# Rotation sublayer of a two-layer decoder: from two batches of sixteen sequences to three batches, and later rotations

## The chip, the core and the metric

The kernel runs on one core of a Trainium2 chip. The core has a matrix engine (TensorE, "PE" in the profile, with its weight loads as "PEld"), a vector engine (VectorE, "DVE"), an activation engine (ScalarE, "ACT"), a general engine (GpSimd, "POOL") and SyncE ("SP"), which here does nothing but issue DMAs; ACT and POOL issue some DMAs as well. Every engine works through its own list of instructions in order, and waits where an instruction needs what another engine or a DMA has not yet delivered. The metric is the device time of one execution in microseconds (us), lower is better.

## What is computed

The input is 32 sequences of 128 tokens with 256 features, in f32, and every matrix product is done in f32. Two decoder layers follow each other. Layer 0 is an attention, a retention with a context, and a routed feed-forward with 8 experts. Layer 1 is the rotation sublayer that is changed here, then an attention with 16 heads, then a second routed feed-forward. The rotation sublayer, per sequence:

```python
h   = layernorm(x)                               # 128 x 256, per token
m   = h.mean(over the 128 tokens)                # one row of 256
om  = skew(m @ omega_proj_w.T + omega_proj_b)    # 64 x 64, antisymmetric
G   = I + om + om^2/2 + om^3/6                   # a rotation, by its series
vi  = m @ vq_in.T + b                            # 64; nearest of 64 codes by cosine
vq  = code[argmax] @ vq_out.T + b
y   = h + omega_mix * ((h[:, :64] @ G) @ omega_out_w.T + b) + vq_mix * vq
x   = x + rmsnorm(y) * norm_w
```

The attention after it needs, for each sequence, queries from `layernorm(x)` with the x that the rotation left; its keys and values come from the context and are ready long before.

## The kernel before

The 32 sequences lie in eight groups of four (`NG`, `GB`); group g is one tile x[g] of 128 tokens x 4 x 256. The stages follow each other: A and B (layer 0's attention and retention), C (layer 0's experts), then D and E together (rotation and attention), and F (layer 1's experts).

**Stage D** (`stage_d`, L1374) begins when stage C's last rows are out. It fetches what the experts made (1 MB for each group, L471, on SP) and the weights of omega in two halves of 2 MB (L1156, on SP). For each group `Dispatch.add` (L488, L489, DVE) sums them into x, and `Lie.measure` takes the layernorm statistics (L173 to L175 on DVE, the root on POOL at L146, a shift at L183). `Lie.means` (L1185) then takes the mean over tokens on PE: for each sequence and each half of the features one product with the 128 x 128 block of x as the weights and one column moving (L1194), and a product with ones for the shift (L1199). All this is done for half of the groups (16 sequences), and `Lie.omegas` (L1201) follows for that half: omega is 64 x 64 numbers a sequence, made in eight parts of 512 columns (L1220, weights 128 x 16), each copied out of PSUM by ACT (L1225) and written to a table in DRAM by SP (L1226); between the parts stand the steps that choose the code and add its row to the output weights `wob` (L1231 to L1273). The second half's means and parts are handed out one piece a step by a generator, `rest()`.

**Turned** (L1279) is the rotation of one group, and its parts are called in different steps: the constructor fetches omega from the table with the sequence index moved inward (L1286, SP), `norm` (ACT, L190), `head` (transposes on PE, L1336) and `square` (DVE L1308, L1309, then PE L1300), `cube`, `spin` (L1345), and `add`, which multiplies with `wob` (L1358), adds and normalises on DVE, ACT and POOL (L1360 to L1367) and adds the result to x (L1371).

**Group** (L1436) makes the queries of one group: its statistics, `norm` (ACT, into one of the two buffers with the tag "h"), `turn` (eight transposes, L239, and two copies), and `queries(h)` for each half h of the features: two products of 512 columns (L1456), an ACT copy (L1461), and eight DMAs on SP (L1464) that place 16 rows each in the tile qT. **Seq** is the attention of one sequence: `largest` (L1478, 16 products on qT, and DVE's maxima, L1485), `less` (L1491, L1493), `scores` (L1501, exponentials on ACT, L1502), `values` (L1509) and `back` (L1519, L1524, L1526).

**The order** around the change is PE's, written out by hand in `step(b)` (L1541), called for b = -13 to 32. Step b does `largest` of sequence b+1, then what is due of queries, turns, rotations and `rest`, then `values` of sequence b-1, `scores` of sequence b, `back` of b-1 and `less` of b+1. A part with the lag n is due for group G in step 4G+n. The other engines' lists come from the scheduler, which follows PE's order; SP's list too. The buffers with tag "h" are shared by the groups' norm, omega's copied parts, and others; there are two. Routing for stage F (`RouteF`: DVE's `rank` with L336 and L338, and `place` on PE with L354 and L355) joins from step 5 on. The lags before:

```python
for n in (-4, -3): ... q.queries(n + 4)          # one half h in each step
if q := due(groups, -5): q.turn()
for n, what in ((-9, "add"), (-10, "spin"), (-11, "cube"), (-12, "head"), (-12, "square")):
```

Of the kernel before, what the change touches and what calls it, by code (L numbers as in the profile page):

```python
# [28 lines left out]
P = 128  # L29
# [242 lines left out]
class Dispatch:  # L272
# [211 lines left out]
    def add(self, g, yg, behind=None):  # L484

        for i in range(0, GB, 2):
            x, y = self.k.x[g][:, i : i + 2, :], yg[:, i : i + 2]
            self.k.order(self.nc.vector.tensor_add(y[:, :, 0, :], y[:, :, 0, :], y[:, :, 1, :]).ins, behind)  # L488
            self.nc.vector.tensor_add(x, x, y[:, :, 0, :])  # L489
# [626 lines left out]

class Lie:
# [3 lines left out]
    def __init__(self, k, p1):  # L1121
        nc = k.nc
        self.k, self.nc, self.p1 = k, nc, p1
        self.w, self.line, self.stats, self.sums = {}, {}, {}, []

    def load(self):
# [5 lines left out]
        for name, shape in shapes.items():  # L1132
            self.w[name] = self.tile(shape, name)
            nc.scalar.dma_start(out=self.w[name], in_=k.ins[name])

# [33 lines left out]
    def length(self, v, n, name):  # L1169

        nc = self.nc
        sq = self.tile([n, OM], f"sq{name}")
        ss = self.tile([n, 1], f"ss{name}")
# [6 lines left out]
    def measure(self, g):  # L1180
        k = self.k
        st = k.stats(g, pool=self.p1, name=f"d_{g}")
        self.stats[g] = st + (k.shift(st, self.p1, f"d_{g}"),)

    def means(self, g):  # L1185

        k, nc = self.k, self.nc
        if g % (NG // 2) == 0:
            self.sums.append(k.bank([P, NC + 1, B // 2]))
        sums, st = self.sums[-1], self.stats[g]  # L1190
        for i in range(GB):
            b = g % (NG // 2) * GB + i
            for c in range(NC):
                nc.tensor.matmul(  # L1194
                    sums[:, c, b : b + 1], lhsT=k.x[g][:, i, c * P : (c + 1) * P], rhs=st[1][:, i : i + 1],
                    start=True, stop=True,
                )
        b -= GB - 1
        nc.tensor.matmul(sums[:, NC, b : b + GB], lhsT=k.deal.ones, rhs=st[2], start=True, stop=True)  # L1199

    def omegas(self, half, pd):  # L1201


        k, nc, w = self.k, self.nc, self.w
        N, HB = 8, B // 2
        tile = lambda shape, name: self.tile(shape, f"{name}{half}")
        mu = tile([P, HB], "mu")
        sums = self.sums[half]
        nc.scalar.activation(mu, sums[:, NC], AF.Copy, scale=1.0 / P)
        hm = tile([P, NC, HB], "hm")  # L1210
        nc.vector.scalar_tensor_tensor(
            hm, sums[:, 0:NC], 1.0 / P, mu.unsqueeze(1).to_broadcast([P, NC, HB]), ALU.mult, ALU.add
        )
        line = self.line[half] = pd.tile([HB, OM, OM], F32, name=f"d_line{half}")

        def part(n):
            po = k.bank([HB, N, OM], "s")
            i = n * N % (OM // 2)
            for c in range(NC):
                nc.tensor.matmul(  # L1220
                    po, lhsT=hm[:, c, :], rhs=self.wu[:, 2 * n * N // OM, c, i : i + N, :],
                    start=c == 0, stop=c == NC - 1,
                )
            rows = k.lnp.tile([HB, N, OM], F32, name="d_rows", tag="h")
            self.copied = nc.scalar.copy(rows, po).ins  # L1225
            nc.sync.dma_start(out=line[:, n * N : (n + 1) * N], in_=rows)  # L1226

        yield part(0)
        pT = k.bank([OM, HB])
        for c in range(NC):  # L1230
            nc.tensor.matmul(pT, lhsT=w["vin"][:, c, :], rhs=hm[:, c, :], start=c == 0, stop=c == NC - 1)  # L1231
        viT = tile([OM, HB], "viT")
        nc.vector.tensor_scalar_add(viT, pT, w["vibc"])
        pvi = k.bank([HB, OM])
        for c in range(NC):
            nc.tensor.matmul(pvi, lhsT=hm[:, c, :], rhs=w["vin"][:, c, :], start=c == 0, stop=False)
        k.bias_mm(pvi, "D_vib", HB)
        vi = tile([HB, OM], "vi")
        nc.vector.tensor_copy(vi, pvi)
        rn = self.length(vi, HB, f"v{half}")  # L1240
        if half == 0:
            self.codes()
        yield part(1)
        psc = k.bank([HB, OM])
        nc.tensor.matmul(psc, lhsT=viT, rhs=self.cbT, start=True, stop=True)
        sc = tile([HB, OM], "sc")
        nc.vector.tensor_scalar_mul(sc, psc, rn)
        best = tile([HB, 1], "best")
        nc.vector.tensor_reduce(best, sc, AX.X, ALU.max)
        nc.vector.tensor_scalar(sc, sc, best, -float(OM), ALU.is_equal, ALU.mult)  # L1250
        nc.vector.tensor_add(sc, sc, w["iota"])
        nc.vector.tensor_reduce(best, sc, AX.X, ALU.min)
        nc.vector.tensor_scalar(sc, sc, best, None, ALU.is_equal)
        yield part(2)
        yield part(3)
        yield part(4)
        ph = k.bank([OM, HB])
        nc.tensor.transpose(ph, sc, k.ident[0:HB, 0:HB])
        hot = tile([OM, HB], "hot")
        nc.vector.tensor_copy(hot, ph)  # L1260
        yield part(5)
        pcode = k.bank([OM, HB])
        nc.tensor.matmul(pcode, lhsT=w["code"], rhs=hot, start=True, stop=True)
        vo = tile([OM, 2 * HB], "vo")
        nc.gpsimd.memset(vo, 0.0)
        nc.vector.tensor_sub(vo[:, 0:HB], pcode, viT)
        nc.vector.tensor_add(vo[:, 0:HB], viT, vo[:, 0:HB])
        yield part(6)
        pvc = k.bank([P, D])
        own = slice(OM + 2 * half * HB, OM + 2 * (half + 1) * HB)  # L1270
        nc.tensor.matmul(pvc[own], lhsT=vo, rhs=w["vout"], start=True, stop=False)
        k.bias_mm(pvc[own], "D_vob", 2 * HB)
        self.known = nc.vector.scalar_tensor_tensor(  # L1273
            w["wob"][own], pvc[own], w["mix"][own, 1:2], w["wob"][own], ALU.mult, ALU.add
        ).ins
        yield part(7)


class Turned:  # L1279


    def __init__(self, lie, g, pool):
        self.lie, self.k, self.nc, self.g, self.pool = lie, lie.k, lie.nc, g, pool
        self.om = self.full("om")
        half, first = divmod(g * GB, B // 2)
        self.fetched = self.nc.sync.dma_start(  # L1286
            out=self.om[0:OM], in_=lie.line[half][first : first + GB].rearrange("b i j -> i b j")
# [17 lines left out]
    def square(self):  # L1305
# [3 lines left out]
        nc.vector.tensor_mul(om, om, over(w["sign"]))  # L1309
# [64 lines left out]
def stage_d(k, lie, pool, pd, room):  # L1374


    half = NG // 2
    weights = lie.weights(pool)
    ygs, last = {}, None

    def fetch(g):
# [601 lines left out]
```

## Time and profile before

| | us |
|---|---|
| median of 17 runs (lowest, highest) | 1670.62 (1667.23, 1677.04) |
| the profiled execution, by its own time | 1672.54 |
| its span, first to last instruction | 1670.80 |
| stage C's last product ends | 1013.1 |
| `largest` of sequence 0 begins (step -1) | 1133.3 |
| `largest` of sequence 7 begins (step 6) | 1200.85 |
| PE busy, whole span | 1441.9 (86%) |
| PE busy from 1013 to 1133 | 89.3 of 120.0 |
| PE busy from 1133 to 1200.85 | 52.4 of 67.85 |
| the four steps 10 to 13, and 14 to 17 | 40.61 and 40.24 |

The page's views name a line of the kernel, an engine, and "out<-in" by the program's tile names. In a timeline the columns are the start in us, the duration in us, the engine and line, the operation, and how many instructions were merged; what stands in brackets is how long the engine had been idle before, and which line of which engine ended that. "PEclk" is the TensorE clock granted, as a share of full speed.

### The profile page before, as it was taken

What the parts mean: (1) busy time and instruction counts of PE and PEld (TensorE: products, weight loads), DVE (VectorE), ACT (ScalarE), POOL (GpSimd) and SP (SyncE); (2) the same over time, 40 slices, a digit from 0 to 9 for tenths busy, and PEclk for the clock granted to TensorE, in tenths of its full rate; (3) what the DMA queues carried; (4) which work ended last, traced back from release to release, by engine and by line L of the source; (5) the groups of instructions that cost most, each with busy time, mean ns of one, the idle gap of its engine ahead of it and who ended that gap; (6) DMA issues with size and microseconds to landing.
All of it is one profiled execution on the core that took longest, in us unless ns stands there. A gap on an engine that the chain in (4) does not pass through costs nothing.

```text
span 1670.8 us, 27093 instructions
## 1 busy us (share of the span) xinstructions
PE 1441.9 (86%) x9161; PEld 958.5 (57%) x9161; DVE 930.6 (56%) x3005; ACT 593.7 (36%) x1524; POOL 603.6 (36%) x621
## 2 busy tenths in 40 slices
PE   6999799999998479999999995796998887878873
PEld 4555577776677446666666664453555544456762
DVE  6666446777778533333333324544767776554566
ACT  2544333334434022222222221143675543433431
POOL 2111126667768721111111114121223543375553
PEclk8999999999999689999999996777999977789997
DMA  9991099911000921111111106300000121043486
GB/s 335 335 335 38 22 309 303 297 43 40 27 20 32 384 67 46 47 48 45 45 45 45 48 29 266 118 9 23 23 14 26 40 96 38 20 136 112 142 264 233
DMA packets 139947, 189.90 MB, mean 114 GB/s; under 512 B 14394, under 2 KB 118148, under 8 KB 137764
## 3 DMA queue, kind: packets, MB, share of 16 engines
q1 hardware_dynamic: 123188, 148.32, 29.3%
q0 software_dynamic: 13296, 36.52, 6.0%
q10 hardware_dynamic: 3328, 3.33, 0.6%
q8 instruction: 76, 1.25, 0.3%
q14 instruction: 59, 0.48, 0.1%
HBM read 69.54 MB, written 112.30 MB: 109 GB/s over the span
## 4 chain that ended last, share of the span: by engine, by line
PE 65%; DVE 14%; issue 6%; ACT 5%; POOL 5%; DMA 3%; SPq 1%; another core or an unknown queue 1%; POOLq 0%; DVEq 0%; ACTq 0%
PE ps L1068 13%; PE ps L1088 7%; PE ps L156 6%; PE ps L664 3%; PE ps L1501 2%; PE ps L1694 2%; PE ps L1710 2%; PE ps L881 2%; PE ps L897 2%; PE ps L239 2%; PE ps L1081 2%; PE ps L151 2%; DVE ln_st L173 2%; PE ps L840 1%; DVE b_sim L887 1%
## 5 line engine op out<-in xcount | busy, mean ns | idle before, releaser
L1068 PE MATMUL ps<-c_up,c_xT 128*128 x568 | 268.1, 595 | 0.0
L342 POOL DMA_INDIRECT r_ys<-c_yb,r_toi x71 | 67.8, 955 | 353.5 <-DVE r_w L460 313.2
L1068 PEld LDWEIGHTS ps<-c_up,c_xT 128*128 128x128 f32 x568 | 102.9, 191 | 73.6 <-issue 69.1
L1088 PE MATMUL ps<-c_down,c_hid 128*128 x568 | 134.8, 380 | 0.9 <-DVE c_hid L1083 0.9
L1088 PEld LDWEIGHTS ps<-c_down,c_hid 128*128 128x128 f32 x568 | 107.4, 190 | 47.2 <-issue 17.7
L887 DVE TENSOR_TENSOR b_sim<-ps,b_decay 128x512 f32<-128x512 f32 x128 | 79.8, 684 | 80.0 <-PE ps L881 48.5
L146 POOL TENSOR_TENSOR b_rs<-b_var,mhalf 128x16 f32<-128x16 f32 x32 | 93.5, 2922 | 82.9 <-DVE b_var L915 79.8
L1093 ACT ACTIVATE c_yb<-ps,r_w 128x256 f32<-128x256 f32 x71 | 33.7, 474 | 219.0 <-PE ps L1088 219.0
L1083 DVE COPY c_hid<-ps 128x512 f32<-128x512 f32 x71 | 49.1, 691 | 101.4 <-PE ps L1081 101.4
L342 POOL DMA_INDIRECT g_ys<-f_yb,g_toi x78 | 76.1, 975 | 63.0 <-DVE g_to L447 46.6
L146 POOL TENSOR_TENSOR ln_rs<-ln_ve,mhalf 128x4 f32<-128x4 f32 x40 | 40.7, 1020 | 133.3 <-DVE ln_ve L175 133.3
L1485 DVE TENSOR_REDUCE e_pad<-ps 128x4 f32<-128x512 f32 x128 | 82.4, 682 | 11.2 <-PE ps L1478 5.4
L1502 ACT ACTIVATE e_e<-ps 128x512 f32<-128x512 f32 x128 | 66.9, 603 | 46.2 <-PE ps L1501 46.1
L173 DVE BATCH_NORM_STATS2 ln_st<-x 128x6 f32<-128x256 f32 x192 | 74.9, 407 | 10.3 <-DMA x<-in_x_dram 5.5
L1076 DVE TENSOR_TENSOR c_su<-ps,c_su 128x512 f32<-128x512 f32 x71 | 49.1, 692 | 55.3 <-PE ps L1068 55.3
L1531 POOL TENSOR_TENSOR x<-x,e_t 128x256 f32<-128x256 f32 x32 | 23.2, 726 | 142.7 <-DVE e_t L1526 142.6
L1074 ACT ACTIVATE c_su<-ps 128x512 f32<-128x512 f32 x71 | 42.4, 598 | 86.8 <-PE ps L1068 86.8
L342 POOL DMA_INDIRECT r_xs<-c_h,r_rowi x64 | 63.9, 998 | 21.9 <-issue 15.2
L342 POOL DMA_INDIRECT g_xs<-f_h,g_rowi x64 | 62.8, 981 | 21.3 <-issue 16.0
L1694 PE MATMUL ps<-f_rw,f_xT 128*128 x312 | 52.5, 294 | 12.5 <-issue 11.2
L1710 PE MATMUL ps<-f_rw,f_hb 128*128 x156 | 51.2, 412 | 13.5 <-ACT f_hb L1706 11.2
L239 PE MATMUL ps<-ident,h 128*128 128x128 f32 x192 | 34.5, 312 | 32.7 <-ACT h L190 14.5
(385 smaller groups left out, 3275.6 us busy)
## 6 DMA issues: line engine op xcount, KB each, us to landing
g_xs<-r_empty SPq DMA_DIRECT2D x16, 2193.0 KB
r_xs<-r_empty SPq DMA_DIRECT2D x8, 4290.0 KB
f_xb<-g_xs SPq DMA_DIRECT2D x78, 129.0 KB
c_xb<-r_xs SPq DMA_DIRECT2D x71, 130.0 KB
c_up<-in_wxu_dram SPq DMA_DIRECT2D x4, 2048.0 KB
c_yg<-r_ys SPq DMA_DIRECT2D x8, 1024.0 KB
f_yg<-g_ys SPq DMA_DIRECT2D x16, 512.0 KB
x<-in_x_dram SPq DMA_DIRECT2D x8, 512.0 KB
```

The costliest lines, as they stand in the source:

```text
L146: inst = self.nc.gpsimd.tensor_tensor(out, in_, self.mhalf[: in_.shape[0], 0:n], ALU.pow)
L156: self.nc.tensor.matmul(out, lhsT=(xT[c] if isinstance(xT, tuple) else xT[:, c])[:, i * P : (i + 1) * P], rhs=w(c), start=c == 0, stop=c = ...
L173: self.order(nc.vector.bn_stats(st[:, i, :], x[:, i, :]).ins, behind)
L239: nc.tensor.transpose(pt[:, i, :], h[:, i, c * P : (c + 1) * P], self.ident)
L342: inst = self.nc.gpsimd.indirect_dma_start(out=table, out_offset=bass.IndirectOffsetOnAxis(ap=rows, axis=0), in_=src, in_offset=None,).ins
L887: nc.vector.tensor_mul(self.sim[:, r].rearrange("p c s t -> p (c s t)"), ps[r].rearrange("p c s t -> p (c s t)"), decay[:, r].rearrange("p ...
L1068: nc.tensor.matmul(pu, lhsT=self.xT[:, c, :], rhs=weights(self.j, glu.up[2 * c + u]), start=c == 0, stop=c == NC - 1,)
L1088: nc.tensor.matmul(py, lhsT=self.hid[:, f, :], rhs=weights(self.j, glu.down[f]), start=f == 0, stop=f == NF0 - 1,)
L1485: nc.vector.tensor_reduce(slots[:, :, r, HD], ps[r], AX.X, ALU.max, negate=True)
L1502: self.exp_by = nc.scalar.activation(self.e[:, r], ps, AF.Exp, scale=1.0 / 16.0).ins
L1694: nc.tensor.matmul(pu, lhsT=self.xT[:, c, :], rhs=experts.rw1[:, self.at, c, :].rearrange("p n f -> p (n f)"), start=c == 0, stop=c == NC - 1,
L1710: nc.tensor.matmul(po, lhsT=self.hid, rhs=experts.rw2[:, self.at, :].rearrange("p n f -> p (n f)"), start=True, stop=True,)
```

## The change

The sequences are taken in three batches: group 0, groups 1 to 3, groups 4 to 7 (`BATCHES`). `measure` writes the inverse deviations onto the diagonal of a zeroed tile (POOL), so that the mean of a sequence is one product with an m-column weight block and the 256 features moving, all summed into m rows of PSUM; `mean` scales them on ACT and turns them by two transposes. `omega` writes four parts at once, into four groups of 32 output rows of one PSUM bank, twice for a batch, with four DMAs for each. `code` is the rest of the old `omegas`, and its last product uses a row `who` that marks the batch's own rows.

`stage_d` does group 0 by itself, then hands out the rest by steps. The steps begin at -9 and not at -13. All lags move: a rotation's `head` from -12 to -8, `add` from -9 to -5; `turn` from -5 to -3; the queries, in two steps before (-4 and -3), are made in one, -2; omega is fetched three groups ahead and not four. Groups 6 and 7 are fetched in halves into buffers with tag "h", behind the last placement of queries (`lie.placed`). `rest` now runs on through the later steps: batch 1's means are in step -5, batch 2's means in step 1 and its omega in step 2.

```diff
+BATCHES = (0,), (1, 2, 3), (4, 5, 6, 7)
...
+        for n, groups in enumerate(BATCHES):
+            m = len(groups) * GB
+            t = self.tile([P, m, m], f"diag{n}")
+            nc.gpsimd.memset(t, 0.0)
...
     def measure(self, g):
...
+        self.nc.gpsimd.tensor_copy(flat[:, own], st[1])
...
+    def means(self, n):
...
+        for g in BATCHES[n]:
+            _, at = place(g)
+            for i in range(GB):
+                nc.tensor.matmul(
+                    self.sums[:, 0:D], lhsT=diag[:, at + i, :], rhs=k.x[g][:, i, :],
+                    start=at + i == 0, stop=at + i == m - 1,
+                )
+    def mean(self, n):
...
+        nc.tensor.matmul(self.sums[:, D : D + 1], lhsT=nb, rhs=k.deal.ones[:, 0:1], start=True, stop=True)
+        mu = self.tile([B // 2, 1], "mu")[0:m]
+        nc.scalar.activation(mu, self.sums[:, D : D + 1], AF.Copy, scale=1.0 / P)
+        rows = k.lnp.tile([m, D], F32, name="d_mean", tag="h")
+        nc.scalar.activation(rows, self.sums[:, 0:D], AF.Identity, bias=mu, scale=1.0 / P)
+        pt = k.bank([P, NC, m])
+        for c in range(NC):
+            nc.tensor.transpose(pt[:, c, :], rows[:, c * P : (c + 1) * P], k.ident[0:m, 0:m])
+        self.hm = self.tile([P, NC, 32], "hm")
+        nc.gpsimd.memset(self.hm, 0.0)
+        nc.vector.tensor_copy(self.hm[:, :, 0:m], pt)
+    def omega(self, n, pd):
...
+        for r in range(2):
+            po = k.bank([P, N, OM], "s")
             for c in range(NC):
+                for q in range(4):
+                    nc.tensor.matmul(
+                        po[32 * q : 32 * q + 32], lhsT=self.hm[:, c, :], rhs=self.wu[:, r, c, q * N : (q + 1) * N, :],
+                        start=c == 0, stop=c == NC - 1,
+                    )
+            rows = k.lnp.tile([P, N, OM], F32, name="d_rows", tag="h")
+            copied = nc.scalar.copy(rows, po).ins
+            for q in range(4):
+                at = (4 * r + q) * N
+                nc.sync.dma_start(out=line[:, at : at + N], in_=rows[32 * q : 32 * q + m])
...
+    for g in range(4):
+        ygs[g] = fetch(g)
+        if g < 2:
+            load(next(weights))
     lie.load()
...
+    def halves(g):
+        nonlocal last
+        last = lie.placed
+        for first in (0, GB // 2):
+            k.disp.add(g, fetch(g, first, GB // 2), None, first, GB // 2)
         lie.measure(g)
...
+    summed(0)
+    lie.means(0)
+    lie.mean(0)
+    lie.omega(0, pd)
+    first = lie.code(0)
+    next(first)
+    summed(1)
     def rest():
...
+        next(first)
+        last = yield
+        for g in (4, 5):
+            ygs[g] = fetch(g)
+        yield
+        next(first)
+        summed(2)
+        yield
+        next(first)
+        summed(3, lie.signed)
+        yield
+        next(first)
+        yield
+        lie.means(1)
+        lie.mean(1)
+        lie.omega(1, pd)
+        second = lie.code(1)
+        next(second)
+        yield
+        summed(4)
...
+        halves(6)
+        next(second)
+        yield
+        halves(7)
+        yield
+        yield
+        lie.means(2)
+        lie.mean(2)
+        yield
+        lie.omega(2, pd)
+        yield
+        yield from lie.code(2)
...
-                for n in (-4, -3):
-                    if q := due(groups, n):
-                        if q.g:
-                            q.queries(n + 4)
-                        else:
-                            for h in range(NC):
-                                q.queries(h, 2 * n + 8, 2)
-                if q := due(groups, -5):
+                if q := due(groups, -2):
+                    n = GB if q.g else GB // 2
+                    for first in range(0, GB, n):
+                        for h in range(NC):
+                            q.queries(h, first, n)
+                if q := due(groups, -3):
                     q.turn()
-                for n, what in ((-9, "add"), (-10, "spin"), (-11, "cube"), (-12, "head"), (-12, "square")):
+                for n, what in ((-5, "add"), (-6, "spin"), (-7, "cube"), (-8, "head"), (-8, "square")):
...
-                if i == 3 and g + 4 < NG:
-                    turned[g + 4] = Turned(lie, g + 4, pd)
-                    turned[g + 4].norm(exp_by)
-                if i == 1 and 0 <= g + 2 < NG:
+                if i == 3 and g + 3 < NG:
+                    turned[g + 3] = Turned(lie, g + 3, pd)
+                    turned[g + 3].norm(exp_by)
+                if i == 3 and 0 <= g + 2 < NG:
                     groups[g + 2] = Group(g + 2)
-                if q := due(groups, -6):
+                if q := due(groups, -4):
                     q.norm(exp_by)
...
-                for b in range(-13, -1):
+                for b in range(-9, 3):
                     step(b, rest)
```

## The prediction

> **What bounds it now.** First the page's forty slices (41.8 us each): PE's busy tenths and its granted clock.
>
> ```profile
> PE   6999799999998479999999995796998887878873
> ...
> PEclk8999999999999689999999996777999977789997
> ```
>
> Slices 25 to 28 of the forty (1002 to 1170 us) read 5, 7, 9, 6 with clocks 0.6, 0.7, 0.7, 0.7: the passage from stage C to attention is the hole. From there on PE is 8 or 9 tenths busy. The PE timeline names the three long idles of the hole (in brackets: idle before, and who ended it):
>
> ```profile
> 1029.66 3.57 PE L1194 MATMUL ps<-d_rs,x 128*128 128x1 f32 x16 [16.56 <-POOL d_rs L146]
> 1079.18 1.11 PE L1300 MATMUL ps<-d_om 128*64 128x64 f32 x8 [8.72 <-DVE d_om L1309]
> 1145.94 2.80 PE L239 MATMUL ps<-ident,h 128*128 128x128 f32 x8 [9.84 <-ACT h L190]
> ```
>
> The third belongs to group 1's norm, which waits for an "h" buffer that omega's parts hold while their DMAs stand on SP behind the placement of queries:
>
> ```profile
> 1121.51 10.08 SPq L1464 DMA_DIRECT2D e_qT<-e_q  x16
> 1131.69 1.28 SPq L1226 DMA_DIRECT2D d_line<-d_rows  x1
> 1133.07 10.25 SPq L1464 DMA_DIRECT2D e_qT<-e_q  x16
> ```
>
> So SP issues one such DMA in 10.08/16 = 0.63 us. In attention I read the waits of PE, then one round of four steps (10 to 13) in its timeline:
>
> ```profile
> 1235.22 1.42 PE L1478 MATMUL ps<-kp,e_qT 32*128 32x128 f32 x32
> ...
> 1240.07 2.63 PE L1501 MATMUL ps<-e_qm,kp 32*128 32x512 f32 x8 [0.43 <-DVE e_pad L1485]
> ...
> 1244.45 1.17 PE L1478 MATMUL ps<-kp,e_qT 32*128 32x128 f32 x32
> ...
> 1261.09 0.38 PE L354 MATMUL ps<-g_both,r_tri 128*128 128x32 f32 x2 [2.45 <-DVE g_both L336]
> 1263.02 0.64 PE L355 MATMUL ps<-g_cum,r_ones 128*128 128x32 f32 x2 [1.55 <-DVE g_cum L338]
> ...
> 1275.83 1.17 PE L1478 MATMUL ps<-kp,e_qT 32*128 32x128 f32 x32
> ```
>
> Step 10 runs from 1235.22 to 1244.45, the round to 1275.83: 40.6 us. No `largest` (L1478) waits for qT, since the queries were made three and two steps earlier. PE's 4.0 us in step 12 end a chain from step 11's `add` through ACT's squares, POOL's root and DVE.
>
> **The passage, after.** Instructions keep their row's duration; their order is that of the changed program's lists. Group 0's sum starts 1.4 us later than now (1022.8): about ten small memsets more stand on POOL ahead of the root that DVE waits for (0.12 to 0.3 each, rows L1265 and L1145). Sum and statistics 4.2 (rows 1022.79 to 1027, without group 1's instructions among them), root 1.4, diagonal copy 0.2 (between L1265's 0.12 and L1331's 0.6): 1030.2. Means: eight passes of 256 columns at half clock, 3.6 by L1358 (x8, 3.62 to 3.76): 1033.8. The extra links of `mean` (shift, two ACT, two transposes, copy): 1.7 (0.2 to 0.5 each by L1209, L1258, L1260): 1035.5. DVE waits here, and group 1's sum is queued behind. Omega: a call with four column groups is two blocks like L1509, the same 128x32 weights and 512 columns, x8 in 0.99 and twice that at half clock: two calls 7.5 (bounds 4.0, and 14.5 if the groups run one after the other at L1220's 1.89 for four products): 1043.0. ACT has group 1's norm ahead of the second copy, 1044.3; four DMAs of 0.63, landing 1.8, 1048.0; omega's fetch 2.2 (row L1286): 1050.2. Now that fetch is issued at 1070.4. Then DVE 0.9, `square` 1.1, `cube` with its DVE links 2.8, `spin` 1.9, the code row and its DVE link 1.7, `add` 3.7, squares and root 3.3, the sums into x 3.0, by their rows at half clock: 1068.6. Now 1105.0.
>
> Batch 1 stands on PE directly behind `add` (1062.3): 24 passes, 6.4 (bounds 5.2 at full clock, 10.8 at half). The clock: with products of one moving column it stays at 0.50 though PE is busy 10.00 of 10 us (1080 to 1100), and the wide L1358 at 1094.9 brings it back within 5.6; so I take most of the 24 at full clock. hm 1070.7, omega 1074.8, written 1079.7, fetched 1081.9. PE's list has group 1's `square` ahead of group 0's `turn`, so `turn` ends at 1087, and after the copies and one product the first query is with SP at 1091. Its 32 DMAs take 20.2: 1111.2. `largest` of sequence 0 needs the first sixteen and ends near 1102.6 (now 1136.1). Behind all 32 on SP stand the fetches of groups 6 and 7; DVE has their sums and statistics ahead of group 1's statistics, so group 1's norm ends at 1132.7, and PE, with everything else queued behind, stands idle from 1117 to 1131 at `turn`. After that come batch 2's means (32 passes, 8 to 9), 1.0 for two waits on ACT, and in step 2 its omega (4.0). Step 2 begins at 1147.4, step 3 at 1160.8, step 4 at 1169, and with two waits on DVE of 3 to 4 `largest` of sequence 7 (step 6) at 1189; now 1200.85. **Passage: -12 us** (bounds -22, if DVE's order costs nothing and the clock is full; -2, if all is at half clock and every DMA lands in 2.2).
>
> PE's own saving, 18 of 30 us (sixteen times 1.89 against three times 4.0), is no term of its own: nearly all lies beside the idles above. The second weights of stage F (L1648, 2 MB) are fetched four steps later, ahead of group 7's placements on SP: issued in 1.2, first needed 60 us on, taken as 0, up to 5 if they are in the way of the placements.
>
> **Each round, after.** Now the queries of group G stand in step 4G-2 and `largest` needs them first thing in step 4G-1. From the start of step 4G-2: `largest` 1.2; from L1456's start to SP's first issue 2.7 (rows 1153.69 and 1156.42); sixteen issues (the 32 KB form takes 4.98 for eight in SP's timeline from 1156.42), the last starts 9.4 after the first; landing 1.8 (bounds 1.3 to 2.2): 15.2 with the last product. Each of the sixteen products waits for its own DMA. Now this stretch, from `largest` to the end of the next `largest`, takes 1235.22 to 1245.62 = 10.4. PE's own work in it after the change is 1.2+3.6 (queries)+1.0 (`spin`)+0.95 (L156)+1.0+1.1+0.5+0.5 (`values`, `scores`, `back`, `less`)+1.2 = 11.1, so PE waits some 4, with `add`, `values` and `scores` queued behind. **+4.8.**
>
> Then: step 4G-1 loses `turn` and ACT's norm and copies (3 us of ACT ahead of `add`'s squares), and DVE gains the group's statistics (1.7) and a wait for POOL: between -2 and +2, taken as -0.3. Step 4G loses half a query (1.9), but PE there waits 4.0 for DVE, which then becomes 5.9: 0. Step 4G+1 has `turn` for the other half: -0.2. The wait of step 4G-2 on DVE's maxima (0.43 to 1.8) and the half clock behind it (L1501 2.63 for 1.14) are already in the 10.4. Sum of a round 4.3, taken as 4.5 (2.5 to 6).
>
> Groups 3, 4 and 5: 13.5. Group 2 (no routing yet; the stretch is 10.8 now, so +4.4, and the code row of batch 2 0.6): 5. Group 6: the stretch is 11.5 now, +3.7; and since there are four steps fewer ahead, one more rotation stands in steps 20 to 23, 4.9 of PE (L1336, L1300, L1345, L1358) and 6.5 of DVE (L1308 to L1367), of which I take 5 to show (0 to 7). Group 7: 14.7 now (its wait on DVE is 4.65), +0.6. **Rounds: +27.8.**
>
> Sum: 1672.54 - 12 + 28 = 1688.5 on the profiled execution's own scale, which stands 1.9 above the median of the runs shown: **1687 us**.
>
> [...] The row: SP needs 0.63 us for each placement of 32 KB or 16 KB. [...]
>
> **Rivals.** (1) *Faster*: rounds are paced by the chain from `add` to `place`, and PE's wait for qT lies beside it: DVE uses the 4 us to catch up, and step 4G's 4.0 us of waiting shrink as much as step 4G-1's grow. It decides if a round loses under 1.5. For it: DVE is busy only 30.2 of 40.6 us, with waits of its own. Against: that chain starts at `add`, which stands behind the delayed `largest` on PE. With 1 for each of groups 2 to 5, 2 for group 6, 0.6 for group 7: 1672.5-12+6.6-1.9 = 1665. (2) *The passage gains nothing*: DVE's order around the fetches of groups 6 and 7 and batch 2's means cost 10 more. 1687+12 = 1699. (3) *Column groups do not run side by side* with omega's weights: 16 products at 0.45 take 7.2 for 2.0, 10.4 a batch, 31 in all: 1718. L1509 speaks against it. (4) *Balance*: groups 2 to 5 at 2.4, group 6 at 4: 1672.5-12+13.6-1.9 = 1672.
>
> **How the numbers follow.** Forecast 0.58, (1) 0.18, (2) 0.14, (3) 0.04, (4) 0.06. The bounds of the passage and of the rounds give the forecast 1674 to 1701 on their own; the range reaches from the edge of (1) to above (2), and leaves out about 0.16: 1666 to 1704. About 0.2% (3.3 us) is what a measurement of this kernel can tell from no change. Faster 0.18, same 0.06, slower 0.76.
>
> **What would show it.** `largest` of sequence 0 near 1102, of sequence 7 near 1189; in the PE timeline an idle or trickling L1577 (the new line of `largest`) of some 4 us once in four steps, ended by the DMA into qT; SP's sixteen placements 10 us long; rounds of 45 us; L1257 x16 in 2 us at full clock. Wrong, if rounds stay at 40 or `largest` finds qT in place, or if the passage ends later than 1198.

## The result: slower, and by more than was forecast

The changed kernel takes 1721.83 us (median of 8 runs, 1717.62 to 1724.87), the kernel before beside it 1672.58 (46 runs): a ratio of **1.0292 [1.0277, 1.0307]**, slower by 49 us where the prediction's sum, -12 + 28, gave 16. The profiled span is 1716.3 us for 1670.8.

First the page's slices of the changed kernel, PE's busy tenths and its granted clock (42.9 us each).

```profile
PE   6999799999997399999999966768987788878873
...
PEclk9999999999999599999999988678878897789997
```

The hole between stage C and attention is still there (6, 6, 7, 6 in slices 24 to 27), and attention behind it reads 7 to 9 tenths as before. The slices hardly show the loss: attention is a little emptier, and longer.

To say where the time went I cut the span at five marks: the end of stage C's last product, the start of `scores` (L1501 before, L1600 after) of sequences 0, 6, 26 and 31, and the end.

| us | before | after | difference |
|---|---|---|---|
| start to the end of stage C | 1013.1 | 1011.2 | -1.9 |
| passage: to `scores` of sequence 6 | 193.0 | 184.4 | -8.6 |
| (of it, to sequence 0) | (145.9) | (97.8) | (-48.1) |
| rounds: sequence 6 to 26, five rounds | 192.1 | 246.0 | **+53.9** |
| sequence 26 to 31 | 59.0 | 61.9 | +2.9 |
| sequence 31 to the end | 213.6 | 212.8 | -0.8 |

So the passage gained about what was forecast, and every round lost 10.8 us, not 4.5. Of the 53.9 us of the rounds PE stands idle for 22.7 more and is busy for 31.2 more (197.4 us for 166.2): one more rotation is in them, `largest` stretches while it waits, and the granted clock is 0.85 for 0.88. The passage in PE's timeline (brackets: idle before, and who ended it):

```profile
1027.42 3.57 PE L1225 MATMUL ps<-x,d_diag 128*4 128x256 f32 x8 [16.21 <-POOL d_diag L1211]
1032.32 3.64 PE L1257 MATMUL ps<-d_wu,d_hm 128*32 128x512 f32 x32 [0.26 <-DVE d_hm L1245]
...
1046.17 1.11 PE L1347 MATMUL ps<-d_om 128*64 128x64 f32 x8 [4.77 <-DVE d_om L1356]
...
1128.14 2.80 PE L239 MATMUL ps<-ident,h 128*128 128x128 f32 x8 [13.48 <-ACT h L190]
```

All of omega for group 0 is one row of 3.64 us, where 7.5 was taken. The long idle of the old passage, which stood at the turn of group 1, is there again, later in the work and longer (13.48 for 9.84).

One round of the changed kernel, in PE's timeline, steps 14 to 16:

```profile
1285.26 3.70 PE L1555 MATMUL ps<-e_hT,w_wE 128*128 128x512 f32 x8
...
1292.28 1.73 PE L1600 MATMUL ps<-e_qm,kp 32*128 32x512 f32 x6 [0.31 <-DVE e_pad L1584]
...
1296.55 2.04 PE L1577 MATMUL ps<-kp,e_qT 32*128 32x128 f32 x28
1298.80 1.07 PE L1577 MATMUL ps<-kp,e_qT 32*128 32x128 f32 x4 [0.20 <-DMA e_qT<-e_q]
1299.79 2.79 PE L1405 MATMUL ps<-d_wob,d_xr 128*128 128x256 f32 x8
...
1308.97 0.30 PE L1383 MATMUL ps<-ident,d_y 128*64 128x128 f32 x1 [0.30 <-ACT d_y L190]
...
1319.09 0.60 PE L354 MATMUL ps<-g_both,r_tri 128*128 128x32 f32 x2 [6.13 <-DVE g_both L336]
```

Two stops are to be seen. The first: `largest` of the next group's first sequence (L1577) takes 3.3 us for 1.2, its last products behind a DMA into qT, and `add` (L1405) behind it runs at a granted clock of 0.69 (2.79 us; in the kernel before 1.89 at full clock, at 1246.89). From the start of step 14's `largest` (1284.16) to the end of this one it is 15.7 us; 15.2 was forecast. SP's timeline has the placements that it waits for:

```profile
1288.00 9.99 SPq L1563 DMA_DIRECT2D e_qT<-e_q  x16
```

The second: `place` (L354) waits 6.13 us for DVE's `rank`, with `scores` queued behind. DVE's timeline of the same round shows what it was doing:

```profile
1286.84 0.17 DVE L175 TENSOR_SCALAR ln_ve<-ln_mv 128x4 f32<-128x4 f32 x1
1291.46 0.16 DVE L183 SCALAR_TENSOR_TENSOR ln_nb<-ln_mv,ln_rs 128x4 f32<-128x4 f32 x1 [4.45 <-POOL ln_rs L146]
1291.54 2.48 DVE L1584 TENSOR_REDUCE e_pad<-ps 128x4 f32<-128x512 f32 x4
...
1313.22 0.19 DVE L322 TENSOR_REDUCE g_first<-g_m 128x4 f32<-128x32 f32 x1
1316.17 0.16 DVE L183 SCALAR_TENSOR_TENSOR ln_nb<-ln_mv,ln_rs 128x4 f32<-128x4 f32 x1 [2.76 <-POOL ln_rs L146]
...
1318.77 0.18 DVE L336 TENSOR_TENSOR g_both<-g_sel,g_sel 128x32 f32<-128x32 f32 x1
```

and POOL's, just before the second of those waits ended:

```profile
1311.83 0.73 POOL L1630 TENSOR_TENSOR x<-x,e_t 128x256 f32<-128x256 f32 x1 [1.16 <-DVE e_t L1625]
1312.73 1.06 POOL L342 DMA_INDIRECT g_xs<-f_h,g_rowi  x1 [0.17 <-issue]
1314.10 0.96 POOL L342 DMA_INDIRECT g_xs<-f_h,g_rowi  x1 [0.30 <-issue]
1315.09 1.04 POOL L146 TENSOR_TENSOR ln_rs<-ln_ve,mhalf 128x4 f32<-128x4 f32 x1
```

Twice in a round DVE stands still, 4.45 and 2.76 us in these rows, at L183, the *shift* of a layernorm (0.16 us of work), because the root that it needs stands on POOL behind a sum into x and two indirect DMAs (the first time behind L599 to L605 too, 2.5 us). Once that holds up the maxima (L1584), for which `scores` waits; once it stands in the middle of `rank` (L318 to L336). In the kernel before, both statistics of a round were taken in one step, and there the shifts (two in one row, x2) came behind the maxima (L1485). DVE's timeline of before:

```profile
1280.04 0.65 DVE L1485 TENSOR_REDUCE e_pad<-ps 128x4 f32<-128x512 f32 x1
...
1281.34 1.28 DVE L1485 TENSOR_REDUCE e_pad<-ps 128x4 f32<-128x512 f32 x2
...
1284.15 0.24 DVE L183 SCALAR_TENSOR_TENSOR ln_nb<-ln_mv,ln_rs 128x4 f32<-128x4 f32 x2 [1.46 <-POOL ln_rs L146]
```

### The profile page after: what moved, and what is told of

The parts are those of the page before. It is cut to its first block, busy times and chain, and to the rows that moved or that the text cites. A ratio compares the mean times of both kernels' runs of the same rounds, so it can differ in the third digit from the quotient of the medians.

```text
span 1716.3 us, 27064 instructions
## 1 busy us (share of the span) xinstructions
PE 1448.4 (84%) x9144; PEld 954.5 (56%) x9144; DVE 932.8 (54%) x3020; ACT 592.3 (35%) x1520; POOL 607.9 (35%) x643
## 4 chain that ended last, share of the span: by engine, by line
PE 63%; DVE 13%; POOL 8%; issue 7%; ACT 4%; DMA 3%; SPq 2%; another core or an unknown queue 0%; POOLq 0%; DVEq 0%; ACTq 0%
PE ps L1068 13%; PE ps L1088 6%; PE ps L156 5%; PE ps L664 3%; DVE e_pad L1584 2%; PE ps L239 2%; PE ps L1792 2%; PE ps L1808 2%; PE ps L881 2%; PE ps L1600 2%; PE ps L151 2%; PE ps L1081 2%; PE ps L1577 1%; PE ps L897 1%; PE ps L840 1%
## 5 line engine op out<-in xcount | busy, mean ns | idle before, releaser
L1584 DVE TENSOR_REDUCE e_pad<-ps 128x4 f32<-128x512 f32 x128 | 82.5, 684 | 24.3 <-PE ps L1577 23.6
L146 POOL TENSOR_TENSOR ln_rs<-ln_ve,mhalf 128x4 f32<-128x4 f32 x40 | 40.9, 1024 | 128.7 <-DVE ln_ve L175 120.1
L1577 PE MATMUL ps<-kp,e_qT 32*128 32x128 f32 x1024 | 66.1, 320 | 7.3 <-DMA e_qT<-e_q 5.0
L1600 PE MATMUL ps<-e_qm,kp 32*128 32x512 f32 x256 | 56.1, 740 | 11.0 <-DVE e_pad L1584 9.1
L1577 PEld LDWEIGHTS ps<-kp,e_qT 32*128 32x128 f32 x1024 | 52.1, 213 | 21.0 <-DMA e_qT<-e_q 12.7
```

The source lines that it names most:

```text
L146: inst = self.nc.gpsimd.tensor_tensor(out, in_, self.mhalf[: in_.shape[0], 0:n], ALU.pow)
L1577: nc.tensor.matmul(ps[r][:, j, :], lhsT=self.group.qT[rows, j, self.i, :], rhs=self.keys[rows, :], start=True, stop=True,)
L1584: nc.vector.tensor_reduce(slots[:, :, r, HD], ps[r], AX.X, ALU.max, negate=True)
L1600: nc.tensor.matmul(ps, lhsT=self.keys[rows, :], rhs=self.qm[rows], start=True, stop=True)
```

## The experiments

Theory S, at the start: a round lost its time by two stops in series on PE, the placements on SP ahead of `largest`, and the group's statistics in front of `rank`. The rivals stand in the expectations. In each experiment the stretches are read at the marks above. The runs e1 to e12 stand beside runs of the kernel before of 1629 to 1632 us and have 184 to 188 us from sequence 31 to the end, the others stand beside 1673 and have 213 to 220; so ratios are always to the runs of before beside them, and of the stretches only the passage and the rounds are compared across. Those agree where the code is the same (rounds 192.1 before and 191.8 in e8; passage 166.4 in e11 and 166.3 in e15) or nearly so (183.5 in e9 and 183.1 in e14); sequence 26 to 31 does not (59.0 before, 55.9 in e8).

**e1, rank first**

```diff
+                if r := route(11):
+                    r.rank(less_by)
...
-                    groups[g + 2] = Group(g + 2)
+                    groups[g + 2] = Group(g + 2, r and r.disp.ranked)   # k.stats(g, behind)
```

> The changed kernel, but in the last step of a round the routing's rank stands on DVE ahead of the next group's layernorm statistics (DVE's list alone differs in the rounds; PE, ACT and SP keep theirs). Theory S (each round of four steps lost about 10 us by two stops in series on PE: placements on SP ahead of largest, and the statistics, which wait for POOL, standing in front of rank and so of place): place waits 2 to 3 us a round and not 4 to 10, rounds shrink by 3 to 5, in all 1721.8 - 6 x 4 = 1698 (1693 to 1705). Rival Q (only the queue of placements costs; the wait at place is the late add's, and would be as long without the statistics): 1717 to 1722. Rival K (the lower granted clock of the rounds is the cost, the stops are only where it shows): 1712 or more.

Ratio 1.0212 [1.0183, 1.0241]; rounds 229.5 for 246.0. PE's wait at `place` over the five rounds, first the kernel before, then the changed kernel, then e1 (line, who ended it, us in all, times, longest; "issue" is a wait whose end the profile does not explain):

```profile
PE ps L354 <- DVE g_both L336: 6.2, 2, 3.8
...
PE ps L354 <- issue: 2.5, 1, 2.5
```

```profile
PE ps L354 <- DVE g_both L336: 26.2, 4, 9.8
```

```profile
PE ps L354 <- DVE g_both L336: 10.9, 4, 4.3
```

Nearly the whole gain is there (15.3 of 16.5 us); PE's busy time stays (197.4 and 197.2). In microseconds on the scale of 1672.6 e1 stands at 1708 (1703 to 1713), just above its range: 3.3 a round, for 4. Rival Q falls, since the wait shrank though PE's order and the placements are the same. Rival K falls by the profile, since the wait alone gave the gain, at the same busy time; by the time alone it is not quite out, as the interval reaches its 1712.

**e2, half of the placements left out**

```diff
-                for m in range(2 * R):
+                for m in range(2 * R if h == 0 or self.g < 2 else 0):
```

> The changed kernel without the placements of the second half of the features for groups 2 to 7 (half of the heads then work on an earlier group's queries; this work is left out, eight of sixteen DMAs on SP in each round). Theory S and rival Q: largest of the first sequence of a group finds its queries 8 x 0.63 = 5 us earlier, add and all behind it too; 4.5 for each of six groups: 1721.8 - 27 = 1695 (1690 to 1702). Rival P (the rounds are paced from place, whose wait grows as the other shrinks): 1715 to 1722.

This kernel leaves work out, so it tells a time and nothing else; DVE's and ACT's lists shift a little with it. Ratio 1.0186 [1.0148, 1.0223], 1704 on the scale of 1672.6, just above its range; rounds 220.5, 25.5 less, 5.1 a round. Rival P falls. `largest` goes from 40.9 us and 3.8 of waiting in five rounds to 29.3 and 0.6, and `add` from 14.3 to 10.0. Eight issues at 0.63 us are 5.0: the price of the placements was right.

**e5, both of these edits**

> The edits of e1 and e2 together: rank ahead of the statistics, and eight of sixteen placements left out for groups 2 to 7. Theory S: the two stops stand in series and add up: from sequence 6 to sequence 26 204 us (246.0 for the changed kernel, less 16.5 in e1, less 25.5 in e2), ratio to before 1.0292 - 0.0080 - 0.0106 = 1.011 (1.007 to 1.015). What then still divides the rounds from the 192 of before is the one more rotation that runs beside them (5) and a rest. Rival P (one stop hides behind the other, so that the second is worth less): 1.016 or more, 212 us or more.

Ratio 1.0126 [1.0101, 1.0151], within theory S; rounds 212.2, where rival P had them: together 33.8 us, not 42. The two share some 8 us, and 20 over before remain.

**e4, only the queries late, in the kernel before**

```diff
+                late = b >= 4
+                for n in (-2,) if late else (-4, -3):
...
-                if i == 1 and 0 <= g + 2 < NG:
+                if i == (3 if g >= 0 else 1) and 0 <= g + 2 < NG:
...
-                if q := due(groups, -6):
+                if q := due(groups, -4 if late else -6):
```

> The kernel before, with the statistics, norm, turn and queries of groups 2 to 7 alone in the later steps of the change (statistics at the end of step 4G-5, queries in step 4G-2); the rotations keep their early steps, and so does the passage. Theory S: each of six groups loses 4.5 to the placements, and 1 to 2 because the statistics stand ahead of rank, although x is long ready: 1672.6 + 6 x 6 = 1708 (1698 to 1715). Rival A (the rounds lose by the rotation's late add, whose sums the statistics wait for, not by the queries): 1673 to 1685.

Ratio 1.0238 [1.0194, 1.0282], 1712 on the scale of 1672.6; rounds 218.5, +26.4. About half of the rounds' loss comes without any late rotation, so rival A falls as the sole cause. The other half comes with the rest of the change: `place` waits 11.4 us here and 26.2 in the changed kernel. That it is the late `add`, and not the one more rotation in the stretch, is likely but not shown apart.

**e3, the batches with the old lags**

```diff
-                for n, what in ((-5, "add"), (-6, "spin"), (-7, "cube"), (-8, "head"), (-8, "square")):
+                for n, what in ((-9, "add"), (-10, "spin"), (-11, "cube"), (-12, "head"), (-12, "square")):
...
-                for b in range(-9, 3):
+                for b in range(-13, -1):
```

(and the lags of queries, turn, norm and statistics likewise)

> The changed kernel's three batches, means as rows and column groups, with the lags and the first step (-13) of the kernel before. Theory S: the rounds go back to those of before, 40 us each, and what is left is what the batches give the passage alone: 1672.6 - 12 = 1660 (1653 to 1667). Rival B (the passage gained by its shorter lags, not by its batches: four steps fewer stand ahead of sequence 0): 1668 to 1676.

Ratio **0.9871 [0.9841, 0.9901]**: faster than before, and in the middle by more than either theory said (1651 us on the scale of 1672.6; the interval reaches into theory S's range). Passage 170.2, that is 22.8 less than before and 14.2 less than the changed kernel; rounds 189.7. The lags, with what follows from them, cost 1.0292/0.9871 = 1.043. One thing that follows: at the old lags the fetches of groups 6 and 7 come ahead of all placements (e12 tries this by itself).

**e7 and e8, column groups alone and means as rows alone, in the kernel before**

```diff
+            if n % 4:
+                return                      # e7: parts n to n+3 at once
...
+                for q in range(4):
+                    nc.tensor.matmul(
+                        po[32 * q : 32 * q + 32], lhsT=hm32[:, c, :], rhs=self.wu[:, n // 4, c, q * N : (q + 1) * N, :],
```

```diff
+            nc.tensor.matmul(                # e8: means(g), two batches of 16
+                self.sums[-1][:, 0:D], lhsT=self.diag[n][0][:, at + i, :], rhs=k.x[g][:, i, :],
+                start=at + i == 0, stop=at + i == B // 2 - 1,
+            )
```

> The kernel before with omega's parts four at a time in column groups, and nothing else of the change (two batches, means as columns, old lags). The prediction's reason (PE's saving lies beside idle time of PE and is no gain of its own): 0.998 to 1.000. Rival W (PE's work sets the passage): two batches of 15.1 us against two of 4.0: up to 22 us less, 0.987 to 0.991.

> The kernel before with the means as rows, and nothing else of the change: 32 passes of 256 columns for 128 products of one column, and two ACT copies, two transposes and a copy more for each half. The prediction's reason: 0.999 to 1.002 (the links cost 1.7 us, the products lie beside idle time). Rival W: 14 us of one-column products at half clock go, 7 to 14 of passes come, and the clock rises sooner: 0.994 to 0.997.

0.993 [0.9911, 0.9948] and 0.9929 [0.9911, 0.9948]: each is worth more than the prediction's reason allows; e7 falls short of rival W, e8's middle lies beyond it and its interval reaches into it. Both passages take 179.6 us for 193.0, and by their ratios to the runs beside them both gain some 12 us. The gains lie in different places: from stage C's end to `largest` of sequence 0 it is 120.1 us before, 119.8 in e7 and 110.0 in e8. SP's timeline of e7 shows what changed there:

```profile
1095.18 19.90 SPq L1232 DMA_DIRECT2D d_line<-d_rows  x8
1115.18 20.66 SPq L1470 DMA_DIRECT2D e_qT<-e_q  x32
```

Omega's last parts are with SP before group 0's queries and no longer between their placements; the wait of group 1's turn for its norm, 9.84 us before, is gone (the longest of that kind is 3.0). In e8 that wait stays (9.84), and most of the gain is earlier, where the second half's means stand between the links of group 0's rotation. PE's timeline, the last of the means and group 0's `add`, before and then e8:

```profile
1091.04 3.58 PE L1194 MATMUL ps<-d_rs,x 128*128 128x1 f32 x16
...
1094.90 3.76 PE L1358 MATMUL ps<-d_wob,d_xr 128*128 128x256 f32 x8
```

```profile
1074.72 1.90 PE L1205 MATMUL ps<-x,d_diag 128*16 128x256 f32 x8
1076.55 1.99 PE L1371 MATMUL ps<-d_wob,d_xr 128*128 128x256 f32 x8
```

A group's means take 1.90 for 3.58, and `add`, which e8 does not touch, 1.99 for 3.76. From group 0's first `square` to the end of its `add` PE needs 19.5 us before (1079.2 to 1098.7) and 11.8 in e8 (1066.7 to 1078.5).

**e11, both parts, still two batches**

> The kernel before with means as rows and column groups together, still two batches and the old lags. If the savings of e7 and e8 add up, 0.986 (0.984 to 0.988), and the third batch, group 0 alone, is worth nothing beside e3's 0.987. If both save the same idle time, 0.990 to 0.993, and the third batch is worth the rest.

Ratio 0.9862 [0.9838, 0.9886]; passage 166.4, rounds 191.5. The two savings add up, and at the old lags the third batch, group 0 alone, is worth nothing beside e3's 0.9871.

**e6, e3 with `place` behind `scores`**

```diff
-                if r := route(12):
-                    r.place()
                 if this:
                     this.scores()
+                if r := route(12):
+                    r.place()
```

> e3 (three batches, the lags of before), and in step 4G place comes behind scores and not ahead of it, so that scores no longer stand on PE behind the wait for DVE's rank. Theory S: PE waited 14.7 us at place in the 20 steps from sequence 6 to 26 of e3; 2.5 a round goes: 0.987 - 0.010 = 0.977 of before (0.973 to 0.982). Rival D (DVE is what is late, and the wait only moves on to the next instruction that needs it): 0.984 to 0.990.

Ratio 0.9837 [0.9812, 0.9862]; rounds 185.2 for 189.7, 0.9 a round. A small gain between the two expectations, with intervals of e3 and e6 that overlap: part of the wait moves on (at `place` 0.8 us for 8.7, at `scores` 12.8 for 9.8). Between e11 and e15 below the same edit is clear of the noise.

**e12, the fetches of groups 6 and 7 not behind the placements**

```diff
-        last = lie.placed
+        last = turned0[0]          # omega's first fetch
```

> The changed kernel, with the four half fetches of groups 6 and 7 no longer held behind the last placement of group 0's queries on SP (three of the four go out ahead of all 32). If these fetches, and DVE's sums behind them, are what holds group 1's norm back, PE's 13.5 us of waiting at the turn of group 1 shrink by 8 or more, and step 6 comes 5 to 12 us earlier: 1.022 to 1.026. If the buffers of tag h or DVE's order hold it anyway: 1.027 to 1.031.

Ratio 1.0266 [1.0234, 1.0297] for 1.0292 [1.0277, 1.0307]: the intervals overlap. Inconclusive in time. In the profile it is not: PE's wait at the turn of group 1 falls from 13.48 us to 2.34, and the passage is 9.4 us shorter (175.0), both as expected of the fetches; the rounds are 3.4 longer (249.4). So the fetches behind the placements did hold group 1's norm back.

**e9, rotations, statistics and queries one step earlier, and e10, that with `place` behind `scores`**

```diff
-                if q := due(groups, -2):
+                if q := due(groups, -3):
...
-                for n, what in ((-5, "add"), (-6, "spin"), (-7, "cube"), (-8, "head"), (-8, "square")):
+                for n, what in ((-6, "add"), (-7, "spin"), (-8, "cube"), (-9, "head"), (-9, "square")):
...
-                if i == 3 and 0 <= g + 2 < NG:
+                if i == 2 and 0 <= g + 2 < NG:
```

> The changed kernel with its later half of the chain one step earlier: rotations -9 to -6 and not -8 to -5, statistics at the end of step 4G-6, norm -5, turn -4, queries -3, first step -10. Placements then have a whole step (about 10 us) before largest needs them, and the statistics no longer stand in the step of rank. Theory S (two stops, both from where the steps collide): sequences 6 to 26 take 192 of before, 5 to 8 for the one more rotation and up to 5 for a rest, 197 to 205 us for 246; ratio 1.0292 - 0.027 = 1.002 (0.996 to 1.008). Rival G (late rotations cost in every round, by the work that they put beside attention, whatever the step): 225 us or more, 1.015 or more.

> e9, and place behind scores as in e6. Theory S: what e6 gained over e3 again (4 to 5 us in sequences 6 to 26, some 0.3 per cent), 0.999 (0.993 to 1.005); it stays above e6 (0.984), since the passage of the short lags takes 14 us more up to sequence 6 than that of e3. Rival G: 1.010 or more.

e9: 1.0096 [1.0067, 1.0124], rounds 213.9; e10: 1.0053 [1.0032, 1.0074], rounds 206.9. Between the two theories. `largest` takes 30.5 us without a wait and `place` waits 0.2: both stops of theory S are gone, and 22 us remain. So theory S was not the whole. The step that is long now is `scores` (PE's timeline, then DVE's; 5.06 us for this `scores`, 1.14 for the one at 1260.26):

```profile
1270.53 5.06 PE L1600 MATMUL ps<-e_qm,kp 32*128 32x512 f32 x8 [3.05 <-DVE e_pad L1584]
```

```profile
1269.71 0.16 DVE L183 SCALAR_TENSOR_TENSOR ln_nb<-ln_mv,ln_rs 128x4 f32<-128x4 f32 x1 [4.43 <-POOL ln_rs L146]
1269.79 2.48 DVE L1584 TENSOR_REDUCE e_pad<-ps 128x4 f32<-128x512 f32 x4
```

The shift again, ahead of the maxima. That made theory V, which e13 and e14 test: one short DVE instruction for each norm, which waits for POOL.

**e13 and e14, the shift behind the maxima**, in the changed kernel and in e9. In the changed kernel nothing moves but L183 in DVE's order; in e9 seven shifts in DVE's order (five of them in the five rounds and at their end), and one instruction of ACT's.

```diff
-    def normed_act(self, g, h, stats, behind=None):
+    def normed_act(self, g, h, stats, behind=None, late=None):
...
-        nb = stats[2] if len(stats) > 2 else self.shift(stats)
+        nb = stats[2] if len(stats) > 2 else self.shift(stats, behind=late)
...
-                    q.norm(exp_by)
+                    q.norm(exp_by, nxt and nxt.max_by)
...
-                    r.norm(exp_by)
+                    r.norm(exp_by, nxt and nxt.max_by)
```

> The changed kernel; on DVE the shift of the layernorms (one short instruction per norm, which waits for the root on POOL, and that root stands behind the sum into x and two indirect DMA issues) comes behind the maxima of the step and not ahead of them or amid rank. Theory V (what is left of the rounds' loss is this one wait on an engine that works in order: 2.8 us amid rank in step 4G, 4.4 us ahead of the maxima in step 4G+2): sequences 6 to 26 take 246 less 12 to 25, ratio 1.029 - 0.011 = 1.018 (1.012 to 1.022). Rival E (the rest is the one more rotation, its own chain and the lower clock): 1.025 or more.

> e9 (one step earlier), and the shift behind the maxima as in e13. In e9 both stops of theory S are gone (largest runs through, place waits 0.2 us), yet the rounds take 213.9 for 192; PE waits 12.0 us at scores, for maxima that stand on DVE behind the shift (4.43 us idle on DVE). Theory V: that goes too, 199 to 206 us, ratio 1.0096 - 0.007 = 1.003 (0.998 to 1.006). Rival E: 210 us or more, 1.007 or more.

e13: 1.0231 [1.0199, 1.0264], rounds 237.6. 8.4 us of the 12 to 25. Its parts say why: `place` waits 16.1 us for 26.2, `scores` goes from 37.7 us and 3.2 of waiting to 31.2 and 1.3, and `largest` from 40.9 and 3.8 to 45.9 and 7.6. So 18.5 us are gained and 8.8 of them given back, besides 4.2 by `add` (18.5 for 14.3): with the maxima earlier, PE reaches `largest` earlier, and the placements, which SP issues by its own pace (0.62 us each in the changed kernel), are not there. One stop had stood in the shadow of the other.

e14: **0.9935 [0.9909, 0.9961]**, rounds 193.8 for 213.9: 20 us over five rounds from where instructions of 0.16 us stand. In DVE's timeline of e14 the maxima now run ahead of it:

```profile
1268.22 0.17 DVE L175 TENSOR_SCALAR ln_ve<-ln_mv 128x4 f32<-128x4 f32 x1
1268.30 2.48 DVE L1584 TENSOR_REDUCE e_pad<-ps 128x4 f32<-128x512 f32 x4
...
1272.83 0.16 DVE L183 SCALAR_TENSOR_TENSOR ln_nb<-ln_mv,ln_rs 128x4 f32<-128x4 f32 x1 [0.78 <-POOL ln_rs L146]
```

More than theory V said (1.003), and rival E falls: with all three stops gone the rounds take 1.7 us more than before, the one more rotation included, at a granted clock of 0.91 for 0.88. That is not yet like with like, because the kernel before has its shift where it was (see e16).

**e15 and e16, the best of it: e11 with `place` behind `scores`, and with the shift behind the maxima too**

> e11 (means as rows and column groups, two batches, old lags), and place behind scores as in e6: 0.9862 - 0.0034 = 0.983 (0.980 to 0.986) if what e6 gained over e3 comes again; 0.985 to 0.988 if DVE's lateness only moves on.

> e15, and the shift behind the maxima. With the old lags the shift stands behind the maxima in the steps of the two statistics already, so theory V gives little: 0.982 (0.979 to 0.985). If the wait at the maxima (4.9 us in 20 steps) is the shift's also here: 0.976 to 0.980.

e15: 0.9802 [0.9782, 0.9822], rounds 186.1. e16: **0.9779 [0.9759, 0.9799]**, passage 164.6, rounds 179.4 us: 2.2% faster than before, and the best version that was run. The shift gains also at the old lags: between e15 and e16 two of them move, and the one at the end of the fifth round, which waited 4.32 us for POOL ahead of the maxima, makes most of the 6.7 us in the rounds.

## Why the prediction was right in its sign and wrong in its size

- **Passage -12: right as a number and as a chain, incomplete as a reason.** `largest` of sequence 7 began at 1188.4 (forecast 1189); that of sequence 0 ended at 1098.7 (forecast 1102.6). Counted from the end of stage C the passage is 8.6 us shorter to `scores` of sequence 6 and 10.5 to `largest` of sequence 7, inside its bounds. The stations of its chain came within 5 us (the first `square` at 1046.2 for 1051). But the number is a sum of two larger things that the prediction did not see: the batches' parts are worth -22.8 (e3), and the shorter lags give 14.2 of that back, 9.4 of it by the fetches of groups 6 and 7 (e12), which the prediction had in its chain.
- **"PE's own saving ... is no term of its own": wrong.** By e7 and e8 each of the two parts alone is worth 13.4 us of passage. By their timelines one frees SP and the buffers earlier, the other shortens the means (1.90 for 3.58), with a granted clock of 0.81 for 0.50 between the links of group 0's rotation. The working had priced PE's products against PE's idle time, and not against what their DMAs and their shape hold up.
- **Omega's two calls 7.5: 3.64**, at full clock (1.00); PE idle at the turn of group 1 from 1117 to 1131: it was 1114.7 to 1128.1. Column groups ran side by side, 0.11 us a product for 0.47 of the old form (rival 3 falls).
- **The stretch of the placements, +4.8 a round: right.** It took 15.7 us for the 15.2 forecast, sixteen placements took 9.99 us on SP (0.62 each, where the row of before gave 0.63), and leaving out eight gave 5.1 a round (e2).
- **"Step 4G ... PE there waits 4.0 for DVE, which then becomes 5.9: 0": this step failed**, together with "taken as -0.3" for step 4G-1. The wait for POOL that the statistics bring was named there and priced at nothing. In the changed kernel the shift stands amid `rank` and ahead of the maxima; `place` (L354) waits 26.2 us in five rounds for 8.7 before, and with its second product (L355) PE waits 7.6 us in each of four rounds for 3.7, where 5.9 was taken. e1 takes 16.5 us off by DVE's order alone, 3.3 a round, and e9 with e14 shows that the same instruction, ahead of the maxima, is worth 20 us, 4 a round, where nothing else covers it; in the changed kernel, where the placements cover a part, moving the shifts gives 8.4 (e13).
- The half query that step 4G lost, 1.9, was no gain either: it had stood in front of `head` while ACT made the norm that `head` needs. L1383 now starts one product at a time behind ACT (4.8 us and 3.4 of waiting in five rounds; 1.8 without a wait before, where one rotation fewer is in the stretch).
- **A round 4.5 (2.5 to 6): 10.8.** 53.9 us for the five rounds where 27.2 was the sum. The price of the one more rotation (5) stays unmeasured. In e14 it and all the rest come to 1.7 over before; but e14's edit takes 6.7 off the rounds at the old lags too (e15, e16), so by an estimate from these runs the rest is some 8 like with like, and 5 fits into it.
- Group 7 and the end (+0.6): +2.9 - 0.8.
- Rival (1) had the right chain, from `add` to `place`, and the wrong sign: its waits grew with what was moved in front of them, and did not lie beside the wait for qT but mostly added to it (e5: 33.8 us of 42).

What stays open: how the 8 us that e1 and e2 share divide between their stops, why the rounds of e12 are longer, and how the 20 us that e5 leaves in the changed kernel's own rounds divide. e14 has lost them, but it also moves the whole chain one step earlier.

## What to carry to other kernels

When work is moved to other steps, follow in each engine's list the first instruction that waits for another engine, and ask what is queued behind it: here a shift of 0.16 us that waited for POOL cost 20 us over five rounds (e9 and e14), and DVE's timeline shows it. A step that loses work may lose a cover: before an instruction is counted as saved, see what ran behind it meanwhile. And price the parts of a bundled change one by one: two of these four (means as rows, column groups) were worth 1.4% together, the third nothing at the old lags, and the lags cost 4%.

## What the hardware showed unexpectedly

- The granted clock stayed at 0.50 through products of one column, although PE shows as busy all the time: from group 0's first `square` to its `add` PE was busy 19.40 of 19.40 us before, at 0.50 (in e7, which keeps these products, the same stretch takes as long: 1072.8 to 1092.3 for 1079.2 to 1098.7); with 256-column passes in between (e8) it was busy 11.80 of 11.80 us at 0.81. Both stretches stand behind idle PE, 8.72 and 8.04 us, and both begin with a `square` of 1.11 us; the next one in e8 takes 0.68, before 1.12. Nor did such products lower a clock that was up: it was 1.00 from 1066 to 1070, where L1194 runs too. What makes the difference is not shown; the weight loads were busy 17.61 of the 19.40 us, and 6.19 of the 11.80.
- In four column groups of 32 rows, 32 products of 512 columns took 3.64 us, 0.11 each; four products of the old form with 16 weight columns took 1.89, 0.47 each, all at full clock (1.00).
- Two stops in series in PE's list were not worth their sum: 25.5 and 16.5 us alone, 33.8 together (e2, e1, e5); and moving the shift alone lengthened `largest` and its wait by 8.8 (e13).
